# Message passing on a graph: one scatter product for two halves, and the node part moved into the edge loop

## The chip, the cores and the metric

The kernel runs on one core of one Trainium2 chip. The metric is the device time of one execution in microseconds (us). A core has five engines with queues of their own, each working in order: TensorE (PE; its weight loads are listed apart as PEld), VectorE (DVE), ScalarE (ACT), GpSimd (POOL) and SyncE (SP), which here only issues transfers. PE multiplies: it holds a weight operand and streams a moving operand through it, the result going to PSUM, a small memory of eight banks of 512 float32 columns on 128 partitions. DVE and ACT read PSUM and SBUF. POOL issues the gathers.

## The reference

There are 12,500 nodes and 200,000 edges, sorted by their target, which is not uniform: it is 12,500 times a uniform number squared, so low nodes have more edges. With ssp the softplus minus log 2:

```
gates       = (ssp(edge_state @ We1 + be1) @ We2 + be2) * (1 - sigmoid(5 * (distance - 3.5)))
h           = ssp(concat(x[src], x[dst]) @ Wn1 + bn1) @ Wn2 + bn2
message_sum = zeros.at[dst].add(h * gates)
new         = x + (ssp(message_sum @ Ws1 + bs1) @ Ws2 + bs2)
out         = layernorm(x + new)
```

Features are 64 wide, Wn1 is 128 by 128, and everything is float32.

## The kernel before

**Groups.** The edges are cut into 391 groups of 512, each of two halves of 256 edges; a half has two tiles of 128, so a group has K = 4 tiles. Sorted targets let all edges of one half fall into a window of W = 42 nodes from the half's lowest target, its base.

**Preparation** (lines 221 to 347). DVE finds the base of every half, PE and DVE build a table in HBM with the target's part of the first node layer, in three bfloat16 pieces per node, in four parts of 25 chunks or fewer (`for i in range(PARTS)`, L315). A step of that loop takes four chunks: product (L325), ACT copy (L328), DVE difference (L329), ACT copy (L330), DVE difference (L331), store (L333). After the first part the array of sums, 64 rows by 12,800 nodes, is set to zero and a row of ones below it to one (L336, L337). It is in SBUF all the time.

**Edge loop** (`for i in range(-4, NG + 1)`). The order of the instructions is the program's order; nothing is planned anew. One iteration works on several groups at once, each at another stage. For iteration i, in this order:

- `load(i + 5)` on SP: edge features eT, target positions relT, and two table windows bw at the bases (L127, L129, L135). Seven buffers.
- `gather(i + 19)` on POOL: four indirect DMAs of 128 rows of x by source (L120). Twenty-four buffers, the first twenty groups are gathered ahead of the loop.
- `layer1(i + 1)` on PE: L157, L159, L163, L164 into z, three strips of 256 columns.
- `transposes(i + 2)` on PE (L147) into the PSUM tile tx, one buffer.
- `exps(i + 1)` and `logs(i + 1)` on ACT (L169, L172): softplus of 768 columns. `xcopy(i + 2)` on ACT (L152): tx to SBUF as xT.
- `layer2(i)` on PE (L181, L184, L187) into gh.
- `scatter(i - 1)` on PE (L208): for each half, the messages of two tiles times a one-hot of 42 columns, into the PSUM tile sc, one buffer.
- on DVE: `softplus(i + 1)` (L176), `onehot(i + 1)` (L201), `hcut(i)` (L193), `message(i)` (L197), `window(i - 1)` (L217, twice), `onehot_rows(i + 4)` (L140).

`window` adds a half's 42 columns into the sums at its base, which DVE loads into a register just before (L214).

A `tile_pool` hands out buffers by name. With one buffer, an instruction that writes the next tile waits for the last reader of the tile before. z takes four PSUM banks (two buffers of two), gh two, tx one, sc one.

**After the loop** all engines read a flag, `far_i`, set in the preparation where some half spans more than its window; only then the slow pass for the edges outside runs (`tc.If`, L377). Next comes the node part (L448 to L489): in 25 blocks of 512 nodes, four to a partition, x is loaded (L458), the sums go through Ws1 (L460), softplus (L463 to L467) and Ws2 (L470, L473), twice x is added (L476), and mean and variance are taken (L478 to L482). One Sqrt and one reciprocal (L484, L485) serve all blocks; then every block is scaled (L488) and stored (L489).

Of the kernel before, what the change touches and what calls it, by code (L numbers as in the profile page):

```python
# [24 lines left out]

# [16 lines left out]
P = 128  # L44
D = 64
# [7 lines left out]
AHEAD = 20  # L53
LOADS = 5
CUTOFF = 5.0
EPS = 1e-5
LN2 = 0.6931471805599453
BIG = 30.0


@with_exitstack
def gnn_resnorm_kernel(ctx: ExitStack, tc: tile.TileContext, a: dict, out: bass.AP):
# [20 lines left out]
    def gh_tile():  # L83
        return psum.tile([P, NB], F32, name="gh")

    rel_d = dram.tile([NR * P, HE], BF16, name="rel_d")
    low_d = dram.tile([NR, P], F32, name="low_d")
# [7 lines left out]
    far_i = const.tile([1, 1], I32, name="far_i")  # L95
    sums = const.tile([D + 1, WIDE], F32, name="sums")
    consts = const.tile([P, P + K * W + 1], F32, name="consts")
    ident = consts[:, :P]
    iota = consts[:, P : P + K * W].rearrange("p (k w) -> p k w", k=K)
    third = consts[:WP, P + K * W :]  # L100
    one = const.tile([P, 1], F32, name="one")
# [9 lines left out]
    wn2 = const.tile([P, D], F32, name="wn2")  # L111
    ws1 = const.tile([D + 1, D], F32, name="ws1")
    ws2 = const.tile([D, D], F32, name="ws2")

# [29 lines left out]
    def transposes(g):  # L144
        tx = psum.tile([P, 2, P], F32, name="tx", bufs=1)
        for t in range(2):
            nc.tensor.transpose(tx[:, t, :], xgs[g][:, 2 * t : 2 * t + 2, :].rearrange("p h f -> p (h f)"), ident)  # L147
        xTs[g] = tx
# [55 lines left out]
    def scatter(g):  # L204
        sc = psum.tile([D, 2, W], F32, name="sc", bufs=1)
        for h in range(2):
            for t in range(2):
                nc.tensor.matmul(sc[:, h, :], msgs[g][:, 2 * t + h, :], ohs[g][:, 2 * t + h, :],  # L208
                                 start=t == 0, stop=t == 1)
        scs[g] = sc  # L210

    def window(g):
        for h in range(2):
            base = nc.values_load(base_i[0:1, 2 * g + h : 2 * g + h + 1], engines=[DVE], min_val=0, max_val=N - 1,  # L214
                                  skip_runtime_bounds_check_because="it was clamped to these bounds")
            part = sums[:D, bass.ds(base, W)]
            nc.vector.tensor_add(part, part, scs[g][:, h, :])  # L217

    with tc.manual_schedule():
# [4 lines left out]
        with tc.tile_pool(name="prep", bufs=1) as prep:  # L224
# [24 lines left out]
            nc.vector.memset(ones3, 1.0)  # L249
            for t in (we1, we2, wnx):  # L250
                nc.vector.memset(t, 0.0)
# [6 lines left out]
            nc.scalar.dma_start(wn2, a["Wn2"])  # L258
            nc.scalar.dma_start(ws1[:D], a["Ws1"])
            nc.scalar.dma_start(ws1[D : D + 1], a["bs1"].rearrange("(o f) -> o f", o=1))  # L260
            nc.scalar.dma_start(ws2, a["Ws2"])
            brow = prep.tile([1, 4, D], F32, name="brow")
# [20 lines left out]
            nc.vector.tensor_reduce(high, dst_f, AX.X, OP.max)  # L283
            nc.vector.tensor_sub(high, high, low)
            span = prep.tile([P, 1], F32, name="span")
            nc.vector.tensor_reduce(span, high, AX.X, OP.max)
# [3 lines left out]
            nc.vector.tensor_reduce(far, ps[:1, :P], AX.X, OP.max)  # L290
            nc.vector.tensor_scalar(far_i, far, float(W), None, OP.is_ge)

# [20 lines left out]
            nc.vector.tensor_scalar(dist, dist, -1.0, 1.0, OP.mult, OP.add)  # L313
            by_node = table.rearrange("(p c) q f -> p c q f", c=NCH)
            for i in range(PARTS):  # L315
                n = min(CP, NCH - i * CP)
# [4 lines left out]
                for c0 in range(0, n, K):  # L321
                    m = min(K, n - c0)
                    ps = gh_tile().rearrange("p (k f) -> p k f", k=K)
                    for k in range(m):
                        nc.tensor.matmul(ps[:, k, :], xTp[i][:, c0 + k, :], wnb, start=True, stop=True)  # L325
                    tb = prep.tile([P, K, PIECES, 2 * D], BF16, name="tb", bufs=3)
                    r1 = prep.tile([P, K, 2 * D], F32, name="r1", bufs=2)
                    nc.scalar.copy(tb[:, :m, 0, :], ps[:, :m, :])  # L328
                    nc.vector.tensor_sub(r1[:, :m, :], ps[:, :m, :], tb[:, :m, 0, :])  # L329
                    nc.scalar.copy(tb[:, :m, 1, :], r1[:, :m, :])  # L330
                    nc.vector.tensor_sub(tb[:, :m, 2, :], r1[:, :m, :], tb[:, :m, 1, :])  # L331
                    c = i * CP + c0
                    nc.sync.dma_start(by_node[:, c : c + m], tb[:, :m])  # L333
                if i == 0:
                    nc.vector.tensor_copy(base_i, base_b[:1])
                    nc.vector.memset(sums[:D], 0.0)  # L336
                    nc.vector.memset(sums[D : D + 1], 1.0)  # L337
                    for k in range(2):
                        nc.vector.tensor_copy(be3[:, k, :], rows[:, 0, :])
                    for k in range(K):  # L340
                        nc.vector.tensor_copy(row3[:, :, k, :], rows[:, 1:3, :])
                        nc.vector.tensor_copy(rs3[:, k, :], rows[:, 3, :])
                if i == 1:
                    nc.vector.tensor_copy(rel, dst_i)
                    for t in range(2):
                        r = rel[:, :, 2 * t : 2 * t + 2]
                        nc.vector.tensor_sub(r, r, base_b[:, :NH].rearrange("p (g h) -> p g h", h=2))


            for i in range(-4, NG + 1):  # L350
                def at(f, g):
# [6 lines left out]
                if i > 0:  # L358
                    at(gather, i + AHEAD - 1)
                at(layer1, i + 1)  # L360
                at(transposes, i + 2)
                at(exps, i + 1)
# [8 lines left out]
                at(window, i - 1)  # L371
                at(onehot_rows, i + 4)


# [71 lines left out]


    NC = -(-N // NB)  # L448
    nodes = ctx.enter_context(tc.tile_pool(name="nodes", bufs=1))
    yc = nodes.tile([P, NC, K, D], F32, name="yc")  # L450
    var = nodes.tile([P, NC, K], F32, name="var")
    nc.vector.memset(var, 1.0)
    xq = x.rearrange("(q k) d -> q k d", k=K)
    oq = out.rearrange("(q k) d -> q k d", k=K)
    for c in range(NC):
        p = min(P, (N - c * NB) // K)
        xt = nodes.tile([P, K, D], F32, name="xt", bufs=4)
        nc.sync.dma_start(xt[:p], xq[c * P : c * P + p])  # L458
        z = z_tile()[:D, 0, : p * K]
        nc.tensor.matmul(z, ws1, sums[:, c * NB : c * NB + p * K], start=True, stop=True)  # L460
        l = nodes.tile([D, NB], F32, name="l_s", bufs=2)
        ln = l[:, : p * K]
        nc.scalar.activation(ln, z, AF.Abs)  # L463
        nc.scalar.activation(ln, ln, AF.Exp, scale=-1.0)
        nc.scalar.activation(ln, ln, AF.Ln, bias=half[:D], scale=0.5)
        s = nodes.tile([D, NB], F32, name="s_s", bufs=2)
        nc.vector.scalar_tensor_tensor(s[:, : p * K], z, 0.0, ln, OP.max, OP.add)  # L467
        slots = s[:, : p * K].rearrange("f (p k) -> f k p", k=K)
        u = gh_tile()[:p, : K * D]
        nc.tensor.matmul(u, ones3[:, :p], rs3.rearrange("q k d -> q (k d)"), start=True, stop=False,  # L470
                         skip_group_check=True)
        for k in range(K):
            nc.tensor.matmul(u[:, k * D : (k + 1) * D], slots[:, k, :], ws2, start=False, stop=k == K - 1,  # L473
                             skip_group_check=True)
        y = nodes.tile([P, K, D], F32, name="y", bufs=2)
        nc.vector.scalar_tensor_tensor(y[:p], xt[:p], 2.0, u.rearrange("p (k d) -> p k d", k=K), OP.mult, OP.add)  # L476
        mean = nodes.tile([P, K], F32, name="mean", bufs=2)
        nc.vector.tensor_reduce(mean[:p], y[:p], AX.X, OP.add)  # L478
        nc.vector.tensor_scalar(mean[:p], mean[:p], 1.0 / D, None, OP.mult)  # L479
        nc.vector.tensor_sub(yc[:p, c], y[:p], mean[:p].to_broadcast([p, K, D]))  # L480
        nc.vector.tensor_mul(y[:p], yc[:p, c], yc[:p, c])  # L481
        nc.vector.tensor_reduce(var[:p, c, :], y[:p], AX.X, OP.add)  # L482
    nc.vector.tensor_scalar(var, var, 1.0 / D, EPS, OP.mult, OP.add)  # L483
    nc.scalar.activation(var, var, AF.Sqrt)  # L484
    nc.vector.reciprocal(var, var)  # L485
    for c in range(NC):
        p = min(P, (N - c * NB) // K)
        nc.vector.tensor_mul(yc[:p, c], yc[:p, c], var[:p, c, :].to_broadcast([p, K, D]))  # L488
        nc.sync.dma_start(oq[c * P : c * P + p], yc[:p, c])  # L489


def layouts(inputs):
# [27 lines left out]
    out["xT"] = np.ascontiguousarray(np.concatenate([t, np.ones_like(t[:1])]))  # L520
    c = np.zeros((P, P + K * W + 1), np.float32)
    c[:, :P] = np.eye(P)
# [22 lines left out]
```

## Time and profile before

| what | us |
|---|---|
| median of three runs (lowest, highest) | 2129.43 (2128.31, 2131.61) |
| the profiled execution's own time | 2132.24 |
| its span, from the first to the last instruction | 2130.4 |
| first L169 of the loop | 136.15 |
| last L169 of the loop | 1989.58 |
| last window add | 1997.04 |
| first load of the node part | 2000.15 |
| last issue of a store ends | 2126.16 |

The mean granted clock of TensorE is 0.964 of full speed; it is 0.99 or more for most of the loop and 0.50 from 2000 us on. Busy over the span: PE 1971.2 us, PEld 1479.7, DVE 1171.6, ACT 865.1, POOL 1497.9.

How to read it: the page cuts the span into 40 slices of some 53 us and gives each engine's busy share in tenths, with the clock of TensorE. An answer in order of time has start, duration, engine, line, operation, result and operands, the count, and in brackets the idle time before it and what ended it. The ends of matmuls are modelled, so that they overlap; the distance between starts is safer. A wait is put down to the event that came last.

### The profile page before, as it was taken

The numbers are of one execution on the slowest core, as the hardware profiler recorded it, in microseconds if no ns is written. First come the engines' busy times: TensorE is split into PE (matmuls) and PEld (weight loads), VectorE is DVE, ScalarE is ACT, GpSimd is POOL, SyncE is SP. The second block draws the span as 40 slices with busy tenths as digits, with TensorE's granted clock in tenths as the row PEclk, the third lists the DMA queues.
The fourth block names the chain that finished last, engine by engine and source line by source line (L and its number), as shares of the span: only waits on it lengthen the run. The fifth ranks groups of instructions, "written<-read, shape, count | busy, mean of one in ns | idle before, by whom it ended". The sixth has DMA issues, their size and how long they took to land. (4 is left out here: it accounts for less than half of the span.)

```text
span 2130.4 us, 40846 instructions
## 1 busy us (share of the span) xinstructions
PE 1971.2 (93%) x12989; PEld 1479.7 (69%) x12989; DVE 1171.6 (55%) x3041; ACT 865.1 (41%) x1307; POOL 1497.9 (70%) x1568
## 2 busy tenths in 40 slices
PE   3379999999999999999999999999999999999895
PEld 2357777777777777777777767677776766767453
DVE  5635555555555555555555555555554555555466
ACT  2234444444444444444444343434334343434342
POOL 7777777777777777777777777777777777777100
PEclk9999999999999999999999999999999999999755
DMA  6455444444444444444444333333333333333102
GB/s 187 125 149 120 98 100 100 99 98 101 99 98 99 101 99 98 99 100 99 97 100 98 91 93 89 94 92 92 92 91 93 90 94 90 93 90 74 27 30 71
DMA packets 284829, 204.94 MB, mean 96 GB/s; under 512 B 148439, under 2 KB 255615, under 8 KB 284351
## 3 DMA queue, kind: packets, MB, share of 16 engines
q1 hardware_dynamic: 233542, 150.56, 26.4%
q0 software_dynamic: 50048, 51.35, 13.0%
q8 instruction: 106, 1.74, 0.3%
q14 instruction: 113, 0.92, 0.1%
q10 hardware_dynamic: 1020, 0.38, 0.1%
HBM read 188.80 MB, written 13.30 MB: 95 GB/s over the span
## 5 line engine op out<-in xcount | busy, mean ns | idle before, releaser
L120 POOL DMA_INDIRECT xg<-in_x,src_i x1564 | 1497.7, 958 | 482.6 <-issue 354.2
L169 ACT ACTIVATE u<-z 128x768 f32<-128x768 f32 x391 | 316.9, 811 | 1067.0 <-PE z L164 1067.0
L176 DVE SCALAR_TENSOR_TENSOR s<-u,z 128x768 f32<-128x768 f32 x391 | 373.0, 954 | 645.9 <-ACT u L172 640.5
L164 PE MATMUL z<-xT,wnx 128*128 128x256 f32 x1564 | 452.9, 383 | 0.8 <-ACT xT L152 0.8
L187 PE MATMUL gh<-wn,s 128*128 128x64 f32 x3128 | 392.3, 268 | 0.0
L187 PEld LDWEIGHTS gh<-wn,s 128*128 128x128 f32 x3128 | 380.7, 192 | 0.0
L172 ACT ACTIVATE u<-u,one 128x768 f32<-128x768 f32 x391 | 365.6, 935 | 12.7
L164 PEld LDWEIGHTS z<-xT,wnx 128*128 128x128 f32 x1564 | 240.1, 193 | 95.8 <-issue 3.6
L159 PE MATMUL z<-eT,we 128*128 128x256 f32 x782 | 276.4, 435 | 6.8 <-DMA eT<-in_eT 6.8
L184 PE MATMUL gh<-we,s 128*128 128x128 f32 x1564 | 278.3, 301 | 0.7 <-DVE s L176 0.6
L184 PEld LDWEIGHTS gh<-we,s 128*128 128x128 f32 x1564 | 203.8, 190 | 89.4 <-issue 42.2
L208 PE MATMUL sc<-oh,msg 128*64 128x42 f32 x3128 | 258.1, 234 | 1.2 <-DVE sums L217 1.2
L217 DVE TENSOR_TENSOR sums<-sums,sc 64x42 f32 x782 | 149.4, 191 | 170.4 <-DVE sums L217 134.7
L208 PEld LDWEIGHTS sc<-oh,msg 128*64 128x64 f32 x3128 | 211.4, 137 | 27.6 <-DVE sums L217 1.5
L147 PE MATMUL tx<-consts,xg 128*128 128x128 f32 x782 | 179.1, 280 | 45.3 <-DMA xg<-in_x,src_i 43.3
L163 PE MATMUL z<-ohT,bw 126*128 126x256 bf16 x782 | 215.8, 276 | 0.0
L147 PEld LDWEIGHTS tx<-consts,xg 128*128 128x128 f32 x782 | 109.9, 141 | 124.4 <-issue 85.3
L197 DVE TENSOR_TENSOR msg<-gh,h 128x256 f32<-128x256 f32 x391 | 165.9, 424 | 13.4
L193 DVE TENSOR_TENSOR h<-gh,cut 128x256 f32<-128x256 f32 x391 | 162.5, 416 | 0.6 <-PE gh L187 0.6
L159 PEld LDWEIGHTS z<-eT,we 128*128 128x128 f32 x782 | 117.1, 189 | 53.8 <-issue 7.0
L181 PE MATMUL gh<-row,ones 3*128 3x512 bf16 x391 | 150.6, 385 | 0.0
L140 DVE TENSOR_SCALAR ohT<-relT,consts 126x512 bf16<-126x512 bf16 x391 | 137.7, 352 | 12.7 <-DMA relT<-rel_d 12.7
(78 smaller groups left out, 1026.4 us busy)
## 6 DMA issues: line engine op xcount, KB each, us to landing
eT<-in_eT SPq DMA_DIRECT2D x391, 128.0 KB
relT<-rel_d SPq DMA_DIRECT2D x391, 126.0 KB
xg<-in_x,src_i POOLq DMA_INDIRECT x1564
bw<-table SPq DMA_DIRECT2D x782, 31.5 KB
table<-tb SPq DMA_DIRECT2D x23, 384.0 KB
xt<-in_x SPq DMA_DIRECT2D x24, 128.0 KB
out<-yc SPq DMA_DIRECT2D x24, 128.0 KB
xTl<-in_xT SPq DMA_DIRECT2D x3, 812.5 KB
```

The source lines that it names most:

```text
L120: nc.gpsimd.indirect_dma_start(out=xg[:, k, :], out_offset=None, in_=x, in_offset=bass.IndirectOffsetOnAxis(ap=src_i[:, g, k : k + 1], axi ...
L147: nc.tensor.transpose(tx[:, t, :], xgs[g][:, 2 * t : 2 * t + 2, :].rearrange("p h f -> p (h f)"), ident)
L159: nc.tensor.matmul(z[:, 0, :HE], we1.rearrange("a h d -> a (h d)"), eTs[g], start=False, stop=True, skip_group_check=True)
L163: nc.tensor.matmul(zn, bws[g][:, h, :], ohTs[g][:, h, :], start=True, stop=False, skip_group_check=True)
L164: nc.tensor.matmul(zn, wnx[:, h, :], xTs[g], start=False, stop=True, skip_group_check=True)
L169: nc.scalar.activation(us[g], zs[g], AF.Exp)
L172: nc.scalar.activation(us[g], us[g], AF.Ln, bias=one)
L176: nc.vector.scalar_tensor_tensor(ss[g].rearrange("p i t e -> p (i t e)"), us[g], BIG, zs[g], OP.min, OP.max)
L184: nc.tensor.matmul(v[:, 0, t], ss[g][:, 0, t, :], we2, start=False, stop=False, skip_group_check=True)
L187: nc.tensor.matmul(v[:, 1, t, h, :], ss[g][:, 1 + h, t, :], wn2, start=False, stop=h == 1 and t == 1, skip_group_check=True)
L197: nc.vector.tensor_mul(msgs[g], ghs[g][:, 0], hs[g])
L208: nc.tensor.matmul(sc[:, h, :], msgs[g][:, 2 * t + h, :], ohs[g][:, 2 * t + h, :], start=t == 0, stop=t == 1)
```

## The change

**Scatter and sums.** The sums have 128 rows: rows 0 to 63 for the first half of each group, 64 to 127 for the second. The scatter is two products over all 128 message columns (both halves) and 84 one-hot columns; of the result the two diagonal blocks are used. The row of ones is gone. The sums are cleared in pieces of 512 columns, one after each step of the table loop.

**PSUM.** Transposes and scatter take their tile from one name, `ts`, with one buffer. The bank that comes free is `nz`, for a node block.

**Node blocks.** `node_block` returns seven functions. Block b's first product uses Ws1 twice in its rows (for the two row groups of the sums) and works on two sub-blocks of 256 nodes at a time, their 64 features stacked on 128 partitions. The bias is added on DVE. The inverse root is exp(-ln(v)/2) with one correction step on DVE, in place of Sqrt and reciprocal.

**When.** `block_steps` gives for every block the iteration by which its edges are expected to be done, from the square root of its place plus a margin of two. At the end of that iteration the seven functions go into a list, `todo`; each following iteration takes one out (two where twelve or more wait), right after `layer1`. Blocks whose step lies behind the loop, and what is left of `todo`, are issued after it, interleaved. The steps are 82, 114, 140, 161, 179, 196, 212, 226, 240, 253, 265, 277, 288, 299, 309, 319, 329, 338, 347, 356, 365, 374, 382, 390 and 393.

**The check.** The flag is also set where a half's base lies below the end of a block that is already issued by then (`least`, in the constants). The pass behind the flag then also computes all node blocks again.

```diff
+def block_steps(N, NG):
+    return [ceil(NG * sqrt(min(1.0, (b + 1) * NB / N))) + MARGIN for b in range(-(-N // NB))]
...
+    def half_tile():
+        return psum.tile([P, NB], F32, name="ts", bufs=1)
+    def node_tile():
+        return psum.tile([P, NB], F32, name="nz", bufs=1)
...
-    sums = const.tile([D + 1, WIDE], F32, name="sums")
+    sums = const.tile([P, WIDE], F32, name="sums")
...
     def transposes(g):
-        tx = psum.tile([P, 2, P], F32, name="tx", bufs=1)
+        tx = half_tile()[:, :HE].rearrange("p (t e) -> p t e", t=2)
...
     def scatter(g):
-        sc = psum.tile([D, 2, W], F32, name="sc", bufs=1)
-        for h in range(2):
-            for t in range(2):
-                nc.tensor.matmul(sc[:, h, :], msgs[g][:, 2 * t + h, :], ohs[g][:, 2 * t + h, :],
-                                 start=t == 0, stop=t == 1)
+        sc = half_tile()[:, : 2 * W]
+        for t in range(2):
+            nc.tensor.matmul(sc, msgs[g][:, 2 * t : 2 * t + 2, :].rearrange("p h f -> p (h f)"),
+                             ohs[g][:, 2 * t : 2 * t + 2, :].rearrange("p h w -> p (h w)"), start=t == 0, stop=t == 1)
...
-            part = sums[:D, bass.ds(base, W)]
-            nc.vector.tensor_add(part, part, scs[g][:, h, :])
+            part = sums[h * D : (h + 1) * D, bass.ds(base, W)]
+            nc.vector.tensor_add(part, part, scs[g][h * D : (h + 1) * D, h * W : (h + 1) * W])
...
+    def node_block(b, pool, tile_of):
...
+        def hidden():
+            t["y"] = tile3("y")
+            nc.sync.dma_start(t["y"], x[rows, :].rearrange("(q p k) d -> p q k d", q=nq, k=2))
+            t["ps"] = tile_of()
+            t["z"] = t["ps"][:, :HE]
+            for q in range(2):
+                nc.tensor.matmul(t["z"], ws1[:, q].rearrange("f o d -> f (o d)"),
+                                 sums[:, b * NB + q * HE : b * NB + (q + 1) * HE], start=q == 0, stop=q == 1)
+            t["l"] = pool.tile([P, HE], F32, name="l_s", bufs=2)
+            nc.vector.tensor_scalar(t["l"], t["z"], bs1[:, 0:1], BIG, OP.add, OP.min)
+        def logs():
+            nc.scalar.activation(t["l"], t["l"], AF.Exp)
+            nc.scalar.activation(t["l"], t["l"], AF.Ln, bias=half, scale=0.5)
+        def ssp():
+            nc.vector.scalar_tensor_tensor(t["l"], t["z"], bs1[:, 1:2], t["l"], OP.add, OP.max)
+        def layer2():
+            slots = t["l"].rearrange("f (p k) -> f k p", k=2)
+            u = t["ps"][:p, HE:].rearrange("p (q k d) -> p q k d", q=2, k=2)
+            nc.tensor.matmul(t["ps"][:p, HE:], ones3[:, :p], rs3.rearrange("q k d -> q (k d)"), start=True,
+                             stop=False, skip_group_check=True)
+            for k in range(2):
+                nc.tensor.matmul(u[:, :, k, :], slots[:, k, :p], ws2, start=False, stop=k == 1, skip_group_check=True)
+            nc.vector.scalar_tensor_tensor(t["y"], t["y"], 2.0, u[:, :nq], OP.mult, OP.add)
+        def center():
+            mean = small("mean")
+            nc.vector.tensor_reduce(mean, t["y"], AX.X, OP.add)
+            nc.vector.tensor_scalar(mean, mean, 1.0 / D, None, OP.mult)
+            nc.vector.tensor_sub(t["y"], t["y"], mean.to_broadcast([p, nq, 2, D]))
+            t["y2"] = tile3("y2")
+            nc.scalar.activation(t["y2"], t["y"], AF.Square)
+        def variance():
+            v, r = small("var"), small("rstd")
+            nc.vector.tensor_reduce(v, t["y2"], AX.X, OP.add)
+            nc.vector.tensor_scalar(v, v, 1.0 / D, EPS, OP.mult, OP.add)
+            nc.scalar.activation(r, v, AF.Ln)
+            nc.scalar.activation(r, r, AF.Exp, scale=-0.5)
+            t["v"], t["r"] = v, r
+        def store():
+            v, r = t["v"], t["r"]
+            nc.vector.tensor_mul(v, v, r)
+            nc.vector.tensor_mul(v, v, r)
+            nc.vector.tensor_scalar(v, v, -0.5, 1.5, OP.mult, OP.add)
+            nc.vector.tensor_mul(r, r, v)
+            nc.vector.tensor_mul(t["y"], t["y"], r.to_broadcast([p, nq, 2, D]))
+            nc.sync.dma_start(out[rows, :].rearrange("(q p k) d -> p q k d", q=nq, k=2), t["y"])
+        return [hidden, logs, ssp, layer2, center, variance, store]
...
+            for i in range(2):
+                for q in range(2):
+                    nc.scalar.dma_start(ws1[i * D : (i + 1) * D, q, q, :], a["Ws1"])
+                nc.scalar.dma_start(ws2[i * D : (i + 1) * D, i, :], a["Ws2"])
+                nc.scalar.dma_start(bs1[i * D : (i + 1) * D, 0:1], a["bs1"].rearrange("(f o) -> f o", o=1))
...
+            nc.vector.tensor_scalar(high, high, float(1 - W), None, OP.add)
+            early = prep.tile([P, NR], F32, name="early")
+            nc.vector.tensor_sub(early, least, low)
+            nc.vector.tensor_max(high, high, early)
...
+                    n1 = min(NB, WIDE - cleared)
+                    if n1 > 0:
+                        nc.vector.memset(sums[:, cleared : cleared + n1], 0.0)
+                        cleared += n1
                 if i == 0:
                     nc.vector.tensor_copy(base_i, base_b[:1])
-                    nc.vector.memset(sums[:D], 0.0)
-                    nc.vector.memset(sums[D : D + 1], 1.0)
...
                 at(layer1, i + 1)
+                for _ in range(1 if len(todo) < 12 else 2):
+                    if todo:
+                        todo.pop(0)()
                 at(transposes, i + 2)
...
                 at(onehot_rows, i + 4)
+                for b, step in enumerate(steps):
+                    if step == i:
+                        todo += node_block(b, finish, node_tile)
+            last = [node_block(b, finish, gh_tile) for b, step in enumerate(steps) if step > NG]
+            for fs in zip_longest(todo, *last):
+                for f in fs:
+                    if f:
+                        f()
...
-    NC = -(-N // NB)
-    nodes = ctx.enter_context(tc.tile_pool(name="nodes", bufs=1))
...
+        for b in range(NBL):
+            for f in node_block(b, o, node_tile):
+                f()
```

More of the change, by code (lines that the diff above doesn't have):

```diff
@@ L26 @@
 from contextlib import ExitStack
+from itertools import zip_longest
+from math import ceil, sqrt
 import concourse.bass as bass
@@ L54 @@
 LOADS = 5
+MARGIN = 2
 CUTOFF = 5.0
@@ L95, in gnn_resnorm_kernel @@
     far_i = const.tile([1, 1], I32, name="far_i")
-    sums = const.tile([D + 1, WIDE], F32, name="sums")
-    consts = const.tile([P, P + K * W + 1], F32, name="consts")
+    sums = const.tile([P, WIDE], F32, name="sums")
+    consts = const.tile([P, P + K * W + 1 + NR], F32, name="consts")
     ident = consts[:, :P]
     iota = consts[:, P : P + K * W].rearrange("p (k w) -> p k w", k=K)
-    third = consts[:WP, P + K * W :]
+    third = consts[:WP, P + K * W : P + K * W + 1]
+    least = consts[:, P + K * W + 1 :]
     one = const.tile([P, 1], F32, name="one")
@@ L111, in gnn_resnorm_kernel @@
     wn2 = const.tile([P, D], F32, name="wn2")
-    ws1 = const.tile([D + 1, D], F32, name="ws1")
-    ws2 = const.tile([D, D], F32, name="ws2")
+    ws1 = const.tile([P, 2, 2, D], F32, name="ws1")
+    ws2 = const.tile([P, 2, D], F32, name="ws2")
+    bs1 = const.tile([P, 2], F32, name="bs1")
     xgs, eTs, relTs, bws, ohTs = {}, {}, {}, {}, {}
@@ L215, in window, with tile3, small @@
                                   skip_runtime_bounds_check_because="it was clamped to these bounds")
-            part = sums[:D, bass.ds(base, W)]
-            nc.vector.tensor_add(part, part, scs[g][:, h, :])
+            part = sums[h * D : (h + 1) * D, bass.ds(base, W)]
+            nc.vector.tensor_add(part, part, scs[g][h * D : (h + 1) * D, h * W : (h + 1) * W])
+    def node_block(b, pool, tile_of):
+        left = N - b * NB
+        nq = min(2, -(-left // HE))
+        p = min(P, left // 2)
+        assert left >= NB or (nq == 1 and left % 2 == 0)
+        t = {}
+        rows = slice(b * NB, b * NB + nq * p * 2)
+        def tile3(name):
+            return pool.tile([P, 2, 2, D], F32, name=name, bufs=2)[:p, :nq]
+        def small(name):
+            return pool.tile([P, 2, 2], F32, name=name, bufs=2)[:p, :nq]
+        def hidden():
[44 more added lines that the diff above has]
+        return [hidden, logs, ssp, layer2, center, variance, store]
@@ L249, in gnn_resnorm_kernel @@
             nc.vector.memset(ones3, 1.0)
-            for t in (we1, we2, wnx):
+            for t in (we1, we2, wnx, ws1, ws2):
                 nc.vector.memset(t, 0.0)
@@ L258, in gnn_resnorm_kernel @@
             nc.scalar.dma_start(wn2, a["Wn2"])
-            nc.scalar.dma_start(ws1[:D], a["Ws1"])
-            nc.scalar.dma_start(ws1[D : D + 1], a["bs1"].rearrange("(o f) -> o f", o=1))
-            nc.scalar.dma_start(ws2, a["Ws2"])
+            for i in range(2):
[3 more added lines that the diff above has]
+                nc.scalar.dma_start(bs1[i * D : (i + 1) * D, 0:1], a["bs1"].rearrange("(f o) -> f o", o=1))
             brow = prep.tile([1, 4, D], F32, name="brow")
@@ L290, in gnn_resnorm_kernel @@
             nc.vector.tensor_reduce(far, ps[:1, :P], AX.X, OP.max)
-            nc.vector.tensor_scalar(far_i, far, float(W), None, OP.is_ge)
+            nc.vector.tensor_scalar(far_i, far, 0.0, None, OP.is_gt)
+            nc.vector.tensor_scalar(bs1[:, 1:2], bs1[:, 0:1], -LN2, None, OP.add)
             ps = gh_tile()
@@ L314, in gnn_resnorm_kernel @@
             by_node = table.rearrange("(p c) q f -> p c q f", c=NCH)
+            cleared = 0
             for i in range(PARTS):
@@ L347, in gnn_resnorm_kernel @@
                         nc.vector.tensor_sub(r, r, base_b[:, :NH].rearrange("p (g h) -> p g h", h=2))
+        assert cleared >= WIDE
+        with tc.tile_pool(name="finish", bufs=1) as finish:
+            steps = block_steps(N, NG)
+            todo = []
             for i in range(-4, NG + 1):
@@ L445, in gnn_resnorm_kernel @@
                 nc.vector.tensor_scalar(to, to, float(-NB), None, OP.add)
-    NC = -(-N // NB)
-    nodes = ctx.enter_context(tc.tile_pool(name="nodes", bufs=1))
[L450 to L489, printed above, removed]
+        for b in range(NBL):
+            for f in node_block(b, o, node_tile):
+                f()
 def layouts(inputs):
@@ L520, in layouts @@
     out["xT"] = np.ascontiguousarray(np.concatenate([t, np.ones_like(t[:1])]))
-    c = np.zeros((P, P + K * W + 1), np.float32)
+    steps = block_steps(N, NG)
+    least = np.zeros(NR * P, np.float32)
+    for b, step in enumerate(steps):
+        least[2 * step : 2 * NG] = (b + 1) * NB
+    c = np.zeros((P, P + K * W + 1 + NR), np.float32)
+    c[:, P + K * W + 1 :] = least.reshape(NR, P).T
     c[:, :P] = np.eye(P)
```

## The prediction

> **What bounds the kernel now.** I read the page first, then the count of softplus exponentials (L169, one per iteration) in stretches of 100 us, then the order of time of one iteration, last the end of the loop. From the page:
>
> ```profile
> span 2130.4 us, 40846 instructions
> PE   3379999999999999999999999999999999999895
> POOL 7777777777777777777777777777777777777100
> PEclk9999999999999999999999999999999999999755
> PE 5%; DVE 1%; issue 0%; DVEq 0%; ACT 0%
> ```
>
> PE looks full until the last slices, POOL works evenly and stops at slice 37, and the chain that ended last is mostly the node part (L460, L473) on a slow clock. The stretches (busy time of L169 with its count, clock, DMA share, GB/s) split the loop in two:
>
> ```profile
> 900.00:1000.00 100.00, 17.84 (x22) 1.00 0.43 99
> ...
> 1300.00:1400.00 100.00, 16.21 (x20) 0.98 0.38 91
> ```
>
> 22 iterations per 100 us (4.54 us each) until about 1100, then 20 (5.0). Early, PE runs without a gap. Late, the gathers set the pace: four indirect DMAs of 0.958 us with 0.30 between them are 5.03 us an iteration. POOL starts at 3.3 us, PE at 136, so POOL begins ahead by its 24 buffers and PE catches up by 0.48 us an iteration. One early iteration in order of time (start, duration, engine, line; L169 to L169):
>
> ```profile
> 1001.57 0.81 ACT L169 ACTIVATE u<-z 128x768 f32<-128x768 f32 x1 [2.50 <-PE z L164]
> ...
> 1002.41 0.94 ACT L172 ACTIVATE u<-u,one 128x768 f32<-128x768 f32 x1
> ...
> 1003.26 0.35 ACT L152 COPY xT<-tx 128x256 f32<-128x256 f32 x1
> 1003.38 0.95 DVE L176 SCALAR_TENSOR_TENSOR s<-u,z 128x768 f32<-128x768 f32 x1 [1.48 <-ACT u L172]
> ...
> 1003.48 0.66 PE L208 MATMUL sc<-oh,msg 128*64 128x42 f32 x8
> 1004.07 0.28 PE L157 MATMUL z<-ones,be 3*128 3x256 bf16 x1
> ...
> 1005.91 0.38 PE L147 MATMUL tx<-consts,xg 128*128 128x128 f32 x2
> 1005.99 0.19 DVE L217 TENSOR_TENSOR sums<-sums,sc 64x42 f32 x1 [0.34 <-DVE sums L217]
> 1006.10 0.34 DVE L140 TENSOR_SCALAR ohT<-relT,consts 126x512 bf16<-126x512 bf16 x1
> 1006.11 0.81 ACT L169 ACTIVATE u<-z 128x768 f32<-128x768 f32 x1 [2.50 <-PE z L164]
> ```
>
> Call the start of L169 T. Then xT is copied at T+2.04, the second window is added at T+4.61, and the next L147 starts at T+4.34. Today L147 and L208 have tiles of their own, so neither the xT copy nor the window add holds PE. The end:
>
> ```profile
> 1997.04 0.19 DVE L217 TENSOR_TENSOR sums<-sums,sc 64x42 f32 x1 [0.32 <-DVE sums L217]
> 2000.15 13.25 SPq L458 DMA_DIRECT2D xt<-in_x  x6
> ```
>
> The last L169 starts at 1989.58. From there 7.65 us finish the loop, 2.9 pass the branch, and the node part runs from 2000 to 2130.
>
> **What the Trainium skill says.** "TensorE: Matmul & The Clock Gate", LDWEIGHTS: a weight load costs its columns divided by 1.2, so 107 ns for 128, 53 for 64. The trace fits: L187 (128 columns, 64 moving) repeats every 116 ns, L208 (64 columns) every 74. The specification table of that page calls ScalarE and VectorE strict FIFO; the order of time above shows no exception. "PSUM — Partial Sum Buffer", Specifications: eight banks. Before, z holds four, gh two, tx and sc one each; a bank for node blocks is only there if two uses share one. "ScalarE: Activation LUTs", What ACT_TABLE_LOAD costs: 1283 ns a load; L311 shows 1283. All loop functions were served by one table set before; I assume Square is in it too.
>
> **The change part by part.**
>
> *Preparation.* The two memsets of the sums take 10.725 us each and idle 2.6 and 2.7 before them: 26.7 us removed, all on the path (PE waits 27.5 us at L325 for DVE). Twenty-five pieces of 128x512 come instead: 0.43 by the old price per column, 0.54 by that of wnx (272 ns for 256). At 0.5 they add 12.5, in series with the table's DVE chain. Five more small loads on ACT's DMA queue (some 0.6 each) and four small DVE operations sit under the wait for the distances (DVE idle 3.2 until 23.99); uncovered they would cost 3. Net -14: L169 first runs at 122 instead of 136.15, the third 8 later, at 130, as before (144.14).
>
> *Scatter.* Eight instructions at 74 ns (0.59) become four with 128 weight columns and 84 moving. L187's 116 ns gives 0.47, L184's 137 gives 0.55; I take 0.52, since after a wait the first load is not hidden. Gain on PE 0.07; the window adds keep their size, and the gap between them: the register load (L214, 304 ns) begins only when the first add starts.
>
> *The shared tile.* Transposes and scatter alternate in one bank, so two waits appear. The scatter must wait for the xT copy: T+2.04, 0.05 hop (L152 to L164 at 138.24), 0.52 scatter, then 2.04 from L157 to the next L169 = 4.65 an iteration. The transposes must wait for the window adds of the iteration before: 4.61 + 0.05, transposes 0.38 (0.31 unstalled; the stalled one late in the loop took 0.07 longer), layer 2 1.80, scatter 0.52, layer 1 2.04 = 9.40 for two iterations, 4.70 each. Behind both waits stands all of PE, hence layer 1 and the next L169. I take 4.67. Bounds: below, no wait bites and PE runs at 4.54 - 0.12 = 4.42; above, another 0.1 of reload at a wait, 4.75.
>
> *A node block in the loop*, seven steps, one per iteration, each between layer 1 and the transposes in every queue:
> - first product: four instructions of 256 columns at 0.22 to 0.27 (L164, L159), 0.97 from T, so transposes run 0.9 late: +0.86. DVE's add (0.42) ends by T+1.5, before L176 at T+1.81.
> - Exp and Ln of 256 columns (0.35 and 0.41 from L152 and the longer L172): in ACT's 2.5 idle, 0; uncovered 0.8. The softplus on DVE (0.42): in its 1.48 idle, 0.
> - second product: 0.11 + four at 0.137 = 0.66 on PE: +0.35.
> - centring: DVE 0.45 + 0.16 + 0.44 from the end of L140, then Square (0.36) on ACT, ahead of L169 in ACT's queue: L169 starts 1.3 late, so copy, scatter and layer 1 do: +1.2.
> - variance: DVE 0.6, then two small ACT operations of 0.2 after L140's end at T+0.36, again ahead of L169: +1.27.
> - store: five DVE operations, 1.1, in the idle time, 0.
>
> Sum 3.7 a block. Bounds: 1.6 if only PE's work counts, 5 with one hop more at each crossing. The x load and the store move into SP's queue, ahead of later loads. A store holds SP until DVE is there; SP runs three iterations ahead (it waits 541.9 us in all for L159 to free buffers), so load i+6 goes out about T+1.5 and its relT is wanted at the end of iteration i+2, some 12 us later: 0. If that cover were gone, ohT and then layer 1 would wait. Nothing enters POOL's queue; its 3.65 us wait at 133 goes.
>
> Of 25 blocks, 23 finish inside the loop; the steps by the rule are 82, 114, ... 382, 390, so from step 299 on one begins every 8 to 10 iterations.
>
> *Sum.* Last L169: 130 + 388 x 4.67 + 23 x 3.7 = 130 + 1812 + 85 = 2027, against 1989.58: +37.4. Is the gather still late anywhere? POOL's lead starts near 107 us (gather 0 lands near 10, the iteration using it starts near 117), shrinks by 5.03 - 4.67 = 0.36 an iteration and regains 3.7 a block: about 40 us at its least, so no. After the last L169: 7.3 to the last window (7.65 before, in which a landing was awaited); block 24 about 8.9 (2.2 for the products on a cooling clock, 0.8 Exp and Ln, 4.0 DVE, 0.8 Square and small ACT, 1.1 for some ten crossings), 1.5 for block 23's interleaved work; 0.4 store issue, 2.9 branch, 1.5 closing: 22.5 against 140.8: -118.3. Together -80.9: span 2049.5, the profiled execution's 2132.24 becomes 2051.3, and on the median of 2129.43 it is 2048.5.
>
> **Rivals.**
> *Gathers stay the bound.* If the waits bite less (4.55 and 2.5 a block give 1953), the last L169 comes at 1989.6 - 3.65 = 1986, plus 22.5: span 2008.5, median 2007.5. For it: POOL sets the pace today from 1100 on, and PE work falls. Against it: the two cycles above, from durations seen.
> *The handover costs more.* The same place with a cycle of 4.8 and blocks of 4.5: 130 + 1862 + 104 + 22.5 = 2118, median about 2117. For it: each wait crosses engines, and weight loads stop being hidden. Against it: hops are 0.05.
> *Slower.* The shared tile serialises transposes, ACT, scatter and DVE so far that an iteration takes over 4.88 us (388 x 0.21 = 81 more): at 4.95 the median is 2157. For it: the bank alternates twice an iteration. Against it: 0.2 more must come from waits whose parts are all seen.
> *The margin fails* and the repair branch runs: on the reference's inputs every block's edges end at least two steps before its block starts, and the widest half spans 35 of 42 nodes; excluded.
>
> **How the numbers follow.** The forecast with its own range 2022 to 2075 gets 0.58, the gathers 0.24 (2003 to 2022), the dearer handover 0.13, slower 0.04, other 0.01. One in ten is left out on either side: 2007 to 2075. Within 0.2%, about what a measurement of this kernel can tell from no change, hardly any case falls: faster 0.95, same 0.01, slower 0.04.
>
> **What would show it.** L169 counts of 21 to 22 per 100 us early and 19 to 20 late, below the gathers' pace; L208 waiting for xT (L152), the transposes for sums; L169 waiting behind Square and the small Ln; POOL idle late because its buffers are full; first L169 near 122; a tail of about 22 us. Wrong if PE waits for xg late in the loop (gathers bind), or if table loads appear in the loop (2.6 us a pair and block, 59 us).

## The result and the profile after

The changed kernel takes 2112.39 us (median of 8 runs, 2105.03 to 2122.77) against 2130.05 for the kernel before (8 runs, 2128.15 to 2131.61): a ratio of 0.9926, 95% interval 0.9902 to 0.995. It is faster, as forecast, but by 0.7% instead of 3.8%, and outside the range of 2007 to 2075. The profiled execution took 2108.15 us with a span of 2106.3. The runs of the changed kernel lie 17.7 us apart, those of the kernel before 3.5, and the clock goes with them: 0.974 in the shortest, 0.965 in the longest.

From the page of the changed kernel:

```profile
span 2106.3 us, 37882 instructions
...
PE   4489999999999999999999999999999999999997
...
POOL 7777777777777777777777777777777777777200
PEclk9999999999999999999999999999999999999987
...
PE 74%; ACT 10%; DVE 9%; issue 4%; DMA 2%; DVEq 1%; ACTq 0%; SPq 0%
```

The node part at the end is gone, PE is full to the last slices, and PE leads the chain that ended last, spread over the lines of the loop. POOL again stops in slice 38, but what follows has changed: the last gather is issued at 1965.5 and the last softplus exponential (L169 before, L191 now) runs at 2080.1, 115 us later; before it was 10 us. The gathers no longer set the pace anywhere; a chain through PE, ACT and DVE does. The waits of PE name it (engine, line, what was waited for, us in total, times, longest):

```profile
PEld ts L169 <- PE z L186: 116.0, 253, 1.0
PEld ts L229 <- ACT xT L174: 58.4, 84, 1.7
PE ts L229 <- ACT xT L174: 41.6, 35, 1.6
```

The scatter (L229) waits for the xT copy (L174), a wait that the kernel before does not have. In an iteration without a node block, in order of time (T is the start of L191):

```profile
1002.66 0.81 ACT L191 ACTIVATE u<-z 128x768 f32<-128x768 f32 x1 [2.93 <-PE z L186]
...
1004.35 0.35 ACT L174 COPY xT<-ts 128x256 f32<-128x256 f32 x1
...
1004.75 0.68 PE L229 MATMUL ts<-oh,msg 128*128 128x84 f32 x4
...
1005.36 0.28 PE L179 MATMUL z<-ones,be 3*128 3x256 bf16 x1
...
1006.76 0.60 PE L186 MATMUL z<-xT,wnx 128*128 128x256 f32 x2
1007.11 0.20 DVE L238 TENSOR_TENSOR sums<-sums,ts 64x42 f32 x1 [0.36 <-issue]
...
1007.38 0.26 PEld L169 LDWEIGHTS ts<-consts,xg 128*128 128x128 f32 x2 [0.43 <-PE z L186]
1007.39 0.81 ACT L191 ACTIVATE u<-z 128x768 f32<-128x768 f32 x1 [2.69 <-PE z L186]
1007.41 0.42 PE L169 MATMUL ts<-consts,xg 128*128 128x128 f32 x2
```

The copy ends at T+2.04, the scatter starts at T+2.09, layer 1 at T+2.70, the next exponential at T+4.73.

The second new wait stands in the same lines: the transposes (L169) start 0.10 after the second window add (L238) ends, in the median iteration as here. PE loses 0.22 us there: from the start of the last pair of L186 to the transposes it takes 0.655 us in the median, instead of the 0.433 between the same lines of the kernel before. The trace puts this wait down to L186; that the adds end it follows from the 0.10. So both waits of the shared tile bite, and nearly equally. The cycle through the copy alone gives 4.73 us; the one through the adds, from the measured parts, (4.65 + 0.10 + 2.06 + 0.56 + 2.03) / 2 = 4.70, an estimate.

Of the 227 intervals without a block the median is 4.73 us, the mean 4.76. Before, the early iterations took 4.54.

A node block adds to this. The intervals from one exponential to the next, mean over the 23 blocks in the loop: 5.53 where the first product is done, 6.46 where the second product and then the late centring fall, 6.07 where the late variance falls, 5.45 after it. The last number was not expected. It is 4.7 to 4.8 in some blocks and 6.3 to 6.9 in others. One of the latter, in order of time:

```profile
1876.80 0.42 ACT L288 ACTIVATE y<-y 128x256 f32<-128x256 f32 x1 [4.03 <-DVE y L286]
...
1877.12 0.79 ACT L191 ACTIVATE u<-z 128x768 f32<-128x768 f32 x1
...
1879.19 0.68 PE L229 MATMUL ts<-oh,msg 128*128 128x84 f32 x4 [1.19 <-ACT xT L174]
...
1880.01 0.70 PE L181 MATMUL z<-eT,we 128*128 128x256 f32 x2
...
1882.69 0.21 ACT L294 ACTIVATE rstd<-var 128x4 f32<-128x4 f32 x1 [3.56 <-DVE var L293]
...
1883.04 0.79 ACT L191 ACTIVATE u<-z 128x768 f32<-128x768 f32 x1
...
1885.12 0.74 PE L229 MATMUL ts<-oh,msg 128*128 128x84 f32 x4 [1.04 <-ACT xT L174]
...
1886.11 1.22 PE L181 MATMUL z<-eT,we 128*128 128x256 f32 x2
...
1892.24 0.70 PE L181 MATMUL z<-eT,we 128*128 128x256 f32 x2
```

Square (L288) and, an iteration later, the small Ln (L294) and Exp hold the exponential, and PE stands for 1.19 and 1.04 us before the scatter. Then layer 1 takes nearly twice its time (L181 1.22 instead of 0.70) and is normal again in the next pass. After 130 us there are 17 such slow passes in this execution. The clock record has 20 stretches at half clock in the loop, 89 us together: 16 of 3.4 us, three of 6.8 and one of 13.7. The windows (ACT busy on L191 with its count, then clock, DMA share, GB/s) show 19 iterations per 100 us at a clock of 0.97 and less:

```profile
1800.00:1900.00 100.00, 15.32 (x19) 0.97 0.41 94
1900.00:2000.00 100.00, 15.11 (x19) 0.95 0.36 87
```

### The profile page after: what moved, and what is told of

Same layout as the page of the kernel before. It is cut to its first block, busy times and chain, and to the rows that moved or that the text cites. A ratio compares the mean times of both kernels' runs of the same rounds, so it can differ in the third digit from the quotient of the medians.

```text
span 2106.3 us, 37882 instructions
## 1 busy us (share of the span) xinstructions
PE 1956.7 (93%) x11375; PEld 1452.2 (69%) x11375; DVE 1230.6 (58%) x3192; ACT 853.1 (40%) x1355; POOL 1486.9 (71%) x1568
## 4 chain that ended last, share of the span: by engine, by line
PE 74%; ACT 10%; DVE 9%; issue 4%; DMA 2%; DVEq 1%; ACTq 0%; SPq 0%
PE z L186 16%; PE gh L209 11%; PE z L181 11%; PE ts L229 9%; PE gh L206 9%; PE ts L169 5%; PE gh L203 4%; ACT u L191 4%; PE z L185 4%; PE z L179 4%; ACT u L194 3%; DVE s L198 2%; PE nz L261 1%; ACT xT L174 1%; DVE sums L238 1%
## 5 line engine op out<-in xcount | busy, mean ns | idle before, releaser
L191 ACT ACTIVATE u<-z 128x768 f32<-128x768 f32 x391 | 316.3, 809 | 961.8 <-PE z L186 953.6
L186 PE MATMUL z<-xT,wnx 128*128 128x256 f32 x1564 | 464.7, 390 | 0.7 <-ACT xT L174 0.7
L186 PEld LDWEIGHTS z<-xT,wnx 128*128 128x128 f32 x1564 | 246.7, 198 | 100.3 <-issue 10.9
L229 PE MATMUL ts<-oh,msg 128*128 128x84 f32 x1564 | 263.3, 292 | 47.3 <-ACT xT L174 41.6
L181 PE MATMUL z<-eT,we 128*128 128x256 f32 x782 | 282.8, 444 | 7.3 <-DMA eT<-in_eT 7.3
L238 DVE TENSOR_TENSOR sums<-sums,ts 64x42 f32 x782 | 153.8, 197 | 186.7 <-issue 147.5
L229 PEld LDWEIGHTS ts<-oh,msg 128*128 128x128 f32 x1564 | 207.9, 193 | 59.3 <-ACT xT L174 58.4
L185 PE MATMUL z<-ohT,bw 126*128 126x256 bf16 x782 | 220.0, 281 | 0.0
L169 PEld LDWEIGHTS ts<-consts,xg 128*128 128x128 f32 x782 | 107.6, 143 | 134.0 <-PE z L186 116.0
L169 PE MATMUL ts<-consts,xg 128*128 128x128 f32 x782 | 164.7, 292 | 21.8 <-PE z L186 7.2
L162 DVE TENSOR_SCALAR ohT<-relT,consts 126x512 bf16<-126x512 bf16 x391 | 152.2, 389 | 25.9 <-DMA relT<-rel_d 13.1
L181 PEld LDWEIGHTS z<-eT,we 128*128 128x128 f32 x782 | 119.8, 193 | 56.1 <-issue 11.4
```

Of the source, the lines that this page charges most:

```text
L181: nc.tensor.matmul(z[:, 0, :HE], we1.rearrange("a h d -> a (h d)"), eTs[g], start=False, stop=True, skip_group_check=True)
L185: nc.tensor.matmul(zn, bws[g][:, h, :], ohTs[g][:, h, :], start=True, stop=False, skip_group_check=True)
L186: nc.tensor.matmul(zn, wnx[:, h, :], xTs[g], start=False, stop=True, skip_group_check=True)
L191: nc.scalar.activation(us[g], zs[g], AF.Exp)
L229: nc.tensor.matmul(sc, msgs[g][:, 2 * t : 2 * t + 2, :].rearrange("p h f -> p (h f)"), ohs[g][:, 2 * t : 2 * t + 2, :].rearrange("p h w -> ...
```

## Experiments

The questions: is it the shared tile (theory S) or the place of the blocks' ScalarE operations (theory A) that costs the loop its time, and what makes the slow passes.

**Square, Ln and Exp one step later.**

```diff
 def center():
-    t["y2"] = tile3("y2")
-    nc.scalar.activation(t["y2"], t["y"], AF.Square)
 def variance():
+    t["y2"] = tile3("y2")
+    nc.scalar.activation(t["y2"], t["y"], AF.Square)
     v, r = small("var"), small("rstd")
...
-    nc.scalar.activation(r, v, AF.Ln)
-    nc.scalar.activation(r, r, AF.Exp, scale=-0.5)
 def store():
     v, r = t["v"], t["r"]
+    nc.scalar.activation(r, v, AF.Ln)
+    nc.scalar.activation(r, r, AF.Exp, scale=-0.5)
```

> The changed kernel, with Square moved to the head of the variance step and the small Ln and Exp to the head of the store step, so that their inputs are an iteration old and ScalarE does them in its idle time. Theory A (the blocks' ScalarE operations ahead of the softplus exponential hold PE, and the idle PE then loses its clock): the late exponentials of 1.2 us in two iterations of each of 23 blocks go, and the half-clock layer-1 passes that follow with them: some 56 + 25 us less, last exponential near 2000, time 2025 to 2040, clock about 1.0 in the loop. Plain iterations stay at 4.73 us. Theory S (only the shared tile counts): the waits come back elsewhere and the time stays within 10 us of the changed kernel, 2105 to 2120.

2029.84 us (4 runs, 2028.3 to 2030.68), ratio 0.9531 (0.9516 to 0.9547). The last exponential is at 2001.59. The three intervals of a block after its first product are 5.29, 4.73 and 4.74 instead of 6.46, 6.07 and 5.45, and there is no slow pass. Plain iterations stay at 4.73. From the page:

```profile
span 2027.3 us, 37905 instructions
...
PEclk9999999999999999999999999999999999999998
```

Theory A holds for 82 us of the 2112, and theory S's forecast of 2105 to 2120 fails. The same operations cost nothing when their inputs are an iteration old: ScalarE does them while it waits for layer 1.

**A bank each for transposes and scatter.**

```diff
 def transposes(g):
-    tx = half_tile()[:, :HE].rearrange("p (t e) -> p t e", t=2)
+    tx = psum.tile([P, 2, P], F32, name="tx", bufs=1)
...
 def scatter(g):
-    sc = half_tile()[:, : 2 * W]
+    sc = psum.tile([P, 2 * W], F32, name="sc", bufs=1)
...
 def hidden():
...
     nc.vector.tensor_scalar(t["l"], t["z"], bs1[:, 0:1], BIG, OP.add, OP.min)
+    t["zb"] = pool.tile([P, HE], F32, name="zb", bufs=2)
+    nc.vector.tensor_scalar(t["zb"], t["z"], bs1[:, 1:2], None, OP.add)
...
 def ssp():
-    nc.vector.scalar_tensor_tensor(t["l"], t["z"], bs1[:, 1:2], t["l"], OP.add, OP.max)
+    nc.vector.tensor_max(t["l"], t["zb"], t["l"])
 def layer2():
+    t["ps"] = tile_of()
...
-                        todo += node_block(b, finish, node_tile)
+                        todo += node_block(b, finish, gh_tile)
```

> The changed kernel, but transposes and scatter have a bank each, as before, and a node block uses two gh tiles in turn, the biased first product being copied to SBUF by one more VectorE operation; the order of ScalarE's operations stays. Theory S (the wait of the scatter for the xT copy, both in one bank, sets 4.73 us an iteration and lets every late exponential through to PE): plain iterations fall to about 4.56 us until the gathers bind at 5.0, late exponentials are absorbed by the 2 us of slack that the softplus has, the last exponential comes near 1977 and the time is 2000 to 2010. Theory A: late exponentials stop PE all the same, 23 x 2.4 us and the clock losses remain, last exponential near 2030, time 2050 to 2065.

2008.3 us (4 runs, 2006.27 to 2012.54), ratio 0.9434 (0.9418 to 0.945). An early iteration of this kernel (its exponential is L185, copy L168, scatter L223, bias of layer 1 L173):

```profile
299.80 0.93 ACT L188 ACTIVATE u<-u,one 128x768 f32<-128x768 f32 x1
...
300.64 0.35 ACT L168 COPY xT<-tx 128x256 f32<-128x256 f32 x1
...
300.77 0.63 PE L223 MATMUL sc<-oh,msg 128*128 128x84 f32 x4
...
301.33 0.28 PE L173 MATMUL z<-ones,be 3*128 3x256 bf16 x1
...
303.37 0.81 ACT L185 ACTIVATE u<-z 128x768 f32<-128x768 f32 x1 [2.37 <-PE z L180]
```

The scatter starts while the copy still runs, 0.22 before it ends; layer 1 follows after 0.56, and the median iteration is 4.41 us, below the 4.54 of the kernel before. Of that gain of 0.13 us only 0.03 lies in the scatter itself (0.593 to 0.559 us from its start to that of layer 1). The other 0.09 lies just ahead of it, from the start of layer 2's last group of products to the scatter's (0.933 to 0.840): in the kernel before, the scatter's first weight load, of 64 columns, starts 0.20 us after layer 2's last product does, here, with 128 columns, 0.06. Why is not shown. From about iteration 200 on the mean is 4.8 to 5.2 and the gathers set the pace again. The last gather is issued at 1970.42, the last exponential runs at 1978.68. The waits:

```profile
PEld z L180 <- ACT xT L168: 35.5, 38, 1.9
PE tx L163 <- DMA xg<-in_x,src_i: 28.0, 35, 2.5
```

The time is the one that theory S forecast, and theory A's 2050 to 2065 fails. But the late exponentials are not wholly absorbed: PE still waits for late copies (L180), and the three intervals are 6.47, 5.96 and 3.46, against 5.30, 4.48 and 4.64 in the next run, some 1.5 us more a block. They cost the end nothing because the gathers would hold it there anyway.

**Both edits.**

> Both edits together. Theory S and theory A both expect the gathers to bind from some iteration on: last gather issued at about 1966, last exponential ten us later, a tail of 25 us, time 1998 to 2010. If S alone is right it equals the run with own banks within 5 us; if A alone is right it is 45 us or more faster than that run.

2009.06 us (4 runs, 2007.7 to 2010.44), ratio 0.9436 (0.942 to 0.9452): the same as own banks alone, as S expects; with the gathers as the limit in both, it does not tell the theories apart. PE waits for the gathered rows:

```profile
PE tx L163 <- DMA xg<-in_x,src_i: 48.6, 77, 1.9
```

So both edits free PE of more than the gathers leave room for. Either version with own banks beats both kernels; against the kernel before it gains 5.6 to 5.7%.

**The shared tile without blocks.** All 25 blocks after the loop, one after another:

```diff
-            steps = block_steps(N, NG)
+            steps = [NG + 1] * NBL
...
-            last = [node_block(b, finish, gh_tile) for b, step in enumerate(steps) if step > NG]
-            for fs in zip_longest(todo, *last):
-                for f in fs:
-                    if f:
-                        f()
+            for b in range(NBL):
+                for f in node_block(b, finish, gh_tile):
+                    f()
```

> The changed kernel with all 25 node blocks after the loop, one after another (the loop has the 128-row scatter and the shared tile, and no block). Theory S: iterations of 4.73 us from first to last, whether or not blocks are there, until the gathers bind near the end; last exponential 1964 to 1978, clock of PE 0.98 or more in the loop. Theory A: without blocks PE is free and iterations are 4.55 us.

The median interval is 4.73 from the third iteration on, without any block, and the last exponential runs at 1975.56, where the gathers (last one at 1966.02) have nearly caught it. The price of 0.32 us over the 4.41 belongs to the shared tile alone. The whole takes 2188.89 us (one run), because the blocks in turn after the loop take some 200 us.

**The second wait of the shared tile.** The first run's kernel, with the xT copy between exponential and logarithm:

```diff
+                at(xcopy, i + 2)
                 at(logs, i + 1)
-                at(xcopy, i + 2)
```

> The run with ScalarE's block operations an iteration later, with the xT copy moved between the exponential and the logarithm of the same iteration. The scatter's wait for the copy goes (copy ready at T+1.2, scatter natural at T+1.9) and only the second wait of the shared tile is left, the transposes for the window adds, which come 0.35 later: by my sum (4.61 + 0.35 + 0.05 + 0.31 + 1.80 + 0.48 + 2.04) / 2 = 4.82 us an iteration. If that wait is not a bound at all, iterations fall to 4.45.

2044.07 us (one run). The interval before the first block is 4.80 in the mean (most lie between 4.63 and 4.9), against 4.82 by the sum and 4.45 without the wait. So the wait of the transposes for the window adds does bound the loop once the other is gone, and it sits just behind the other one. That 4.82 came so close is partly luck, since its parts are off: the adds end 0.13 later than before the move (T+4.78), not 0.35, the transposes start 0.10 after them, not 0.05, and a scatter that does not wait takes 0.56, not 0.48. With these, (4.78 + 0.10 + 2.06 + 0.56 + 2.03) / 2 = 4.77; the median is 4.78.

**What halves the clock: products on three rows.** The changed kernel with work for PE where it stood:

```diff
+            fill = {s + j for s in steps for j in (5, 6)}
...
                 at(layer2, i)
+                if i in fill:
+                    ps = node_tile()
+                    for _ in range(4):
+                        nc.tensor.matmul(ps, ones3[:, :P], row3.rearrange("q i k d -> q (i k d)"), start=True, stop=True)
                 at(scatter, i - 1)
```

> The changed kernel, with four products of 512 bfloat16 columns (0.32 us each) into the idle node bank put ahead of the scatter in the two iterations of every block in which the softplus exponential is late; their result is used by nobody. PE then works through the 1.0 to 1.2 us in which it stood. If standing still is what halves the clock for the next layer-1 pass (16 such passes in the loop of the changed kernel, some 1.5 us each), they vanish: clock 0.99 in the loop, runs closer to each other, 2085 to 2100 (25 us less, up to 10 given back where the products outlast the wait). If something else slows these passes (a late table window, a transfer), they stay, and the time is 2112 to 2125.

2134.63 us (22 runs, 2117.28 to 2158.02), ratio 1.0015 (1.0 to 1.0029, without the two longest runs): slower than without them, at least as scattered, and outside both ranges. There are 21 slow passes, and the loop spends some 130 us at half clock instead of 89, though PE now stands for 0.5 us at most ahead of the scatter. Taken alone this spoke against the idle time as the cause.

**The same with products on all rows.**

```diff
-                    for _ in range(4):
-                        nc.tensor.matmul(ps, ones3[:, :P], row3.rearrange("q i k d -> q (i k d)"), start=True, stop=True)
+                    for _ in range(3):
+                        nc.tensor.matmul(ps[:, :HE], ident, wnx.rearrange("p h f -> p (h f)"), start=True, stop=True)
```

> As the run with the filler, but with three float32 products of 256 columns on all 128 rows (six instructions of 0.21 us) in place of the four that used three rows. If PE standing, or working with few rows, is what halves the clock afterwards, the slow layer-1 passes go: clock 0.99, 2085 to 2100, runs within 0.3%. If they still stay, standing PE is not their cause, and the time is 2112 to 2140.

2084.85 us (4 runs, 2083.95 to 2086.54), ratio 0.9781 (0.9765 to 0.9798). No slow pass is left, and the runs agree again:

```profile
span 2084.7 us, 38434 instructions
...
PEclk9999999999999999999999999999999999999998
```

Work that nobody uses makes the kernel 27.5 us faster. So the slow passes come from PE having too little to do just before them, and the bfloat16 products on three rows do not count for enough. Whether the rows or the bfloat16 type decide that is not separated: the two fillers differ in both.

**One late exponential.** The changed kernel with only the Ln and Exp moved:

```diff
-    nc.scalar.activation(r, v, AF.Ln)
-    nc.scalar.activation(r, r, AF.Exp, scale=-0.5)
 def store():
     v, r = t["v"], t["r"]
+    nc.scalar.activation(r, v, AF.Ln)
+    nc.scalar.activation(r, r, AF.Exp, scale=-0.5)
```

> The changed kernel with only the small Ln and Exp moved to the next step; Square stays ahead of the softplus exponential. One late exponential in each block is left, 23 x 1.2 us less than the changed kernel. If two stretches of standing PE in a row are needed for the slow layer-1 passes, these go too: 2055 to 2065, clock 0.99. If one is enough, they stay: 2080 to 2090, clock 0.97.

2081.83 us (4 runs, 2073.49 to 2093.09), ratio 0.9786 (0.9758 to 0.9815). This lies in the range forecast for the case that one stand is enough. In the profiled execution, the fastest of the four, 4 slow passes and 7 stretches at half clock are left and the clock is 0.986 (0.974 to 0.981 in the others). One stand of PE can be enough: in the changed kernel, too, 11 of the 20 stretches have only one stand in the 8 us before them. Whether two in a row do it more often is not shown.

## Why the prediction was wrong

The path was right: a chain of PE, ACT and DVE through the shared bank in place of the gathers. Two terms of its sum failed. The iteration was put at 4.67 us and is 4.76, mainly because a scatter that has waited takes 0.61 us and not 0.52; and the half clock after PE has stood was put at nothing and cost 27.5 us.

**What bounds the loop: right.** Both new waits are there, at the places named, and the gathers no longer bind. The forecast that the gain in the node part (118 us) is partly paid back in the loop was right in kind; the loop paid back 90.5 us (last exponential at 2080.1 instead of 1989.58), not 37.4.

**The cycle of the shared tile: mis-sized.** The step took 0.52 for the scatter and 4.67 for an iteration. Measured: 2.09 + 0.61 + 2.03 = 4.73, the mean with some longer iterations 4.76; why those are longer was not looked into. The scatter that starts after a wait takes 0.61, one that does not takes 0.56 (the run with own banks). The step had divided the time of a group by its count, which gave 116 ns for L187 and 74 for L208. But from one product's start to the next it is 112 and 58 ns, and the rest is the handover to the next line: four starts 0.11 to 0.13 apart and 0.21 from the last to layer 1 make the 0.56. 388 x 0.09 = 35 us of the miss; the step's own upper bound, 4.75, would have covered 4.73. The second wait, put at 4.70, comes out at 4.70 from measured parts too, but by errors that cancel (layer 2 takes 1.70 and not 1.80; the hop is 0.10 and not 0.05).

**A node block: right.** Forecast 3.7 us. In the execution with PE kept busy the excess over 4.76 is 0.77 for the first product, 1.71 for second product and centring, 1.17 for the variance: 3.65. Forecast were 0.86, 1.55 and 1.27. Within the second part the product alone costs 0.53 (the run with ScalarE's operations later), not 0.35, so that here too errors cancel.

**The clock: left out.** The sum took layer 1 at full clock throughout and followed the late exponential only to the next wait. It did not ask what PE's standing does to PE. That step failed: 27.5 us by the medians with and without the full-row products. The Trainium skill ("TensorE: Matmul & The Clock Gate", Why this matters for your kernels) warns of idle gaps over some 3 us; here stretches of 1.0 to 1.6 us sufficed, so the measurement decides. The half clock mostly lasts 3.4 us (about 1885.6 to 1889.0 above).

**Preparation: right.** First exponential at 120.37 (forecast 122), third at 128.35 (130). A clearing piece took 0.485 us (forecast 0.5).

**The queues: right.** A store holds SP 16.6 us in the mean (398.9 in 24 waits), and no load came late for it: DVE waited for relT 13.1 us in all, five times, as in the kernel before (12.7, five times).

**The tail: mis-sized.** 26.2 us from the last exponential to the end, forecast 22.5. The two first products ran on the half clock, 1.7 and 2.1 us.

Together: 2049.5 + 35 for the cycle + about 23 for the clock in this execution + 3.7 for the tail - 1.7 for the earlier start - 1 for the blocks = 2108.5; the span is 2106.3.

**The rivals.** "Gathers stay the bound" did not come true, yet its time of 2007.5 is that of the version with own banks. "The handover costs more" (4.8 and 4.5 a block, 2117) came nearest in time. Its cycle is near, and a restart after a wait does cost more; its dearer block is what the clock did and not the handover, so that half of the hit is luck. No table load stands in the loop, so Square was served by the set in use.

## What to carry to other kernels

Two uses of one buffer in turn turn two independent paths into one cycle: add up that cycle before giving a bank away, since here the bank freed cost 0.32 us an iteration and its second user could have lived in another rotating tile. In an engine that works in order, an operation put ahead of the critical one must have inputs that are already old; moved one step later, the same operations cost nothing. And a stall on PE is not over when it ends: look at the duration of the products right after it.

## What the runs showed of the hardware

PE standing for 1.0 to 1.6 us, once or twice within some 6 us, was followed by a stretch at half clock, mostly of 3.4 us, in part of the cases: 20 such stretches in one execution of the changed kernel with two stands a block, 7 with one stand a block, none in the blocks where full-row products filled the stands. They make a kernel's time scatter: 2105 to 2123 with these stands, within 3 us without. Bfloat16 products using three of 128 rows did not keep the clock up.

Stretches at half clock also follow waits for gathered rows: six in the loop of the kernel before, after waits of 0.29 to 1.37 us, and seven in the run with both edits, after waits of 1.03 to 1.94. No run here removes those waits alone, so that they are the cause is not shown. Length alone does not decide: in the run with the block operations later PE waits up to 0.44 us in the loop, and no stretch at half clock follows.

And between two adds at addresses read from memory DVE paused in all 391 pairs of the changed kernel: the second add's register load (303 ns) begins only after the first add has started, 0.03 us in the median, so that 0.34 us or more, 0.36 in the median, lie between them although they touch different rows.
